# A four-layer image kernel: third layer's gates spread by transfers and computed inside the next half image, 3x3 convolutions as a stage of their own

## The chip, the cores and the metric

The kernel runs on one core of one Trainium2 chip, in one launch. A core has five engines that work side by side, each through its own stream of instructions: PE (TensorE, matmuls, with PEld for the loads of its weights), DVE (VectorE), ACT (ScalarE), POOL (GpSimd) and SP (SyncE, which here only issues transfers). They meet through semaphores. Operands lie in SBUF, matmul results in PSUM, and large tensors in HBM, called DRAM in the code. The metric is the device time of one execution in microseconds (us); of several runs the median is given.

## The reference

Four layers follow each other on a batch of four 64x64 images with 128 channels, in float32. The first (layer 0) and second (layer 1) are vision state-space blocks: projections, a depthwise convolution, and scans over the image in four directions; the first also has a branch with two 3x3 convolutions. The fourth is a 7x7 neighborhood attention. The change lies in the third layer (layer 2 in the code) and in the order of the side work of the first two. The third layer is, cut to its core:

```python
norm = _ln(tokens, ln1_w, ln1_b)
neigh = stack of the 9 shifted images of norm           # 3x3 neighbours, zero at the borders
edge = concatenate([center, neigh, center - neigh, relp], axis=-1)
drive = _mlp(edge, d_w1, d_b1, d_w2, d_b2)[..., 0]       # gelu between the two products
resistance = _mlp(edge, r_w1, r_b1, r_w2, r_b2)[..., 0]
gate = sigmoid(clip(lam * drive / (softplus(resistance) + softplus(gamma) + 1e-6), -3, 3) + bias)
values = neigh @ v_w + v_b
message = sum(gate * values, axis=2) / sum(gate, axis=2)
return _ln(tokens + message @ o_w + o_b, ln2_w, ln2_b)
```

## The kernel before, in words

Channels lie on the 128 partitions and pixels along the free dimension. An image has 4096 pixels, in eight chunks of 512 (eight rows). A matmul of 128x512 fills one of PSUM's eight banks.

**Layers 0 and 1.** `Scans.run` walks through 3072 units of scan. A unit is one scan on DVE (`scan`) with its decay (PE and ACT), its product with B (POOL, `times_b`), its product with C (DVE) and sums on PE. All other work of these layers is cut into pieces and slipped between the units: `Side` has a generator per stage (`pre0`, `convs`, `post0`, `pre1`, `post1`) that yields at each piece, `order` lists which stage of which image follows which and before which scan it has to be done, and `between` in `scan_layers` draws pieces from that list at a pace of at least `PACE` = 0.83 per unit, or faster where `PIECES`, the number of pieces that a stage is taken to have, says that a scan would come too early. A piece is only drawn if a small planner (`Plan`, `Lane`) finds room for it on its engine, or if it is late. In the kernel before, `pre0` of the images 1 to 3 holds both the projections with the depthwise convolution (`open0`) and the two 3x3 convolutions (`convs`); image 0's `open0` runs ahead of the scans and its `convs` stand after the three `pre0`.

**Layer 2.** `layer2` records a program by hand; each engine runs it in the order in which it is written. Work goes by half images: image `b`, half `s`, four chunks. `Edges.edges` makes 18 steps for a half: for the drive (m = 0) and the resistance (m = 1) nine neighbours each. A step adds the center's projection `cen` (PSUM, four banks) to the shifted projection of the neighbour `near` (SBUF) in two DVE instructions of 128x1024 (`hid`), passes them through GELU on ACT, and sums over channels on PE into row t of four blocks of 32 partitions (`out0`, `out1`, one bank each). Between steps it calls pieces of other work from the list `side`, spread evenly. After the steps `Edges.gates` turns the two banks into gates in five pieces on DVE and ACT: softplus, division, clip, sigmoid, and the division by the sum of the nine gates (a matmul with `mass`). The first two run alone, the other three mixed with a filling of statistics and projections.

The gates of a half are then used among the steps of the next one, in `Edges.gather`: for each neighbour t and each pair of chunks, PE spreads row t of the gates `g` over all partitions with a matmul against `pick` (L1408), into one of two `mm` banks, DVE multiplies it with the shifted values `vals` (L1414), and POOL adds the product to `acc` (L1418). `vals` is made by `project` with a third matmul per chunk and is kept for two images. The second norm and the store follow (`output` in `gather`, and `finish` one half later). `statistics` and `project` prepare the norm and the projections some chunks ahead; `roots` takes inverse square roots as exp(-0.5 ln) on ACT.

The loops of `layer2`: statistics and projections of the first chunks, then eight halves, then `finish` of the last but one, and gather, roots and `finish` of the last.

Of the kernel before, what the change touches and what calls it, by code (L numbers as in the profile page):

```python
# [531 lines left out]
class Side:  # L532
# [254 lines left out]
    def pre0(self, b):  # L787

        yield from self.open0(b)
        yield from self.convs(b)  # L790

    def open0(self, b):
        nc = self.nc
        wt = self.weights(self.d0a[:, 0 : 3 * P])
        cv12, inp = wt[:, 0:P], wt[0:H, P : 3 * P]
        lo, hi = slice(0, H), slice(H, P)
        x = self.fetch("x", self.x0[b, :, chunk(0)])
        for c in range(NCH):
            yield ("PE", self.landed) if c == 0 else "PE"
            ps = self.bank()  # L800
            nc.tensor.matmul(ps, cv12, x, start=True, stop=True)
            if c + 1 < NCH:
                x = self.fetch("x", self.x0[b, :, chunk(c + 1)])
            yield self.when("TAB", "d0")

            rl = self.tile("d0")
            self.act(rl, ps, AF.Silu, scale=self.cv12g, bias=self.cv12b)
            yield "PE POOL"
            l = self.tile("sq")
            nc.gpsimd.tensor_scalar(l[hi], rl[hi], self.bn0g[hi], self.bn0b[hi], ALU.mult, ALU.add)  # L810
            ps = self.bank()
            nc.tensor.matmul(ps, inp[:, 0:P], rl[lo], start=True, stop=True)
            yield self.when("ACT", "d1")
            xi = self.tile("d1")
            nc.scalar.copy(xi, ps)
            self.store("d1", self.xid[0, b, 0][:, chunk(c)], xi)
            self.store("sq", self.ld[b][0][:, chunk(c)], l[hi])
            yield "PE"
            ps = self.bank()
            nc.tensor.matmul(ps, inp[:, P : 2 * P], rl[lo], start=True, stop=True)  # L820
            yield self.when("TAB", "o")
            sz = self.tile("o")
            self.act(sz, ps, AF.Silu)
            self.store("o", self.szd[0, b, 0][:, chunk(c)], sz)
        yield from self.depthwise(self.dww0, self.dwb0, self.xid[0, b, 0], self.xcd[0, b, 0])

    def convs(self, b):
        nc = self.nc
# [194 lines left out]
PIECES = dict(pre0=157, convs=66, post0=114, pre1=172, post1=290)  # L1023
# [3 lines left out]
def order(nb):  # L1027
# [4 lines left out]
    side = []  # L1032
    for b in range(1, nb):
        side.append(("pre0", b, None, (0, b)))
    side[3:3] = [("convs", 0, None, None), ("post0", 0, (0, 0), None)]
    side.append(("pre1", 0, (0, 0), (1, 0)))
    for b in range(1, nb):
        side += [("post0", b, (0, b), None), ("pre1", b, (0, b), (1, b))]
# [6 lines left out]
def scan_layers(tc, C, nb, x_in, d0, s0, d1, s1, out):  # L1045

    nc = tc.nc
    with ExitStack() as es:
# [48 lines left out]
        with tc.manual_schedule():  # L1097
            for _ in side.open0(0):
                pass
# [20 lines left out]
class Edges:  # L1120
# [9 lines left out]
    def __init__(self, tc, C, es, nb, x_in, x_out, d_w, d_rel, d_v):  # L1130
# [4 lines left out]
        self.psum = es.enter_context(tc.tile_pool(name="l2p", bufs=1, space=PSUM))  # L1135

# [56 lines left out]
        self.pick = wp.tile([P, NB, P], F32, name="pick")  # L1193
        nc.vector.tensor_copy(self.pick, fold[:, 0:NB].unsqueeze(2).to_broadcast([P, NB, P]))
# [20 lines left out]
        self.vals = [[wp.tile([P, HR, PW], F32, name=f"vals{i}{s}") for s in range(2)] for i in range(min(nb, 2))]  # L1215
# [3 lines left out]
        for tiles in self.vals:  # L1219
            for t in tiles:  # L1220
                nc.vector.tensor_copy(t.rearrange("p h w -> p (h w)"), vb.to_broadcast([P, HR * PW]))
# [37 lines left out]
    def project(self, b, c):  # L1259

        nc = self.nc
        n = self.norm[b % 2][:, c, :]
        s, r = divmod(c, 4)

        def scale():
            nc.gpsimd.tensor_mul(n, n, self.rstd[:, c, :])

        def part(i):
            ps = self.bank()
            nc.tensor.matmul(ps, self.vw if i == 2 else self.wnei[:, i, :], n, start=True, stop=True)  # L1270
            tiles = self.vals[b % 2] if i == 2 else self.near[i]
            bias = self.inb[:, i : i + 1]

            def rows(s, first, some):
                to = tiles[s][:, first : first + some.shape[1], 1 : 1 + HW]
                nc.scalar.activation(to, some, AF.Identity, bias=bias)

            rows(s, 1 + r * ROWS, image(ps))


            if c == 3 and i == 2:
                rows(1, 0, image(ps)[:, ROWS - 1 : ROWS, :])
            if c == 4:
                rows(0, HR - 1, image(ps)[:, 0:1, :])

        return [scale] + [lambda i=i: part(i) for i in range(3)]
# [5 lines left out]
    def edges(self, b, s, side):  # L1292

        nc = self.nc
        out = [self.psum.tile([P, T], F32, name="out", tag=f"out{m}", bufs=1) for m in range(2)]
        steps, gone = 2 * NB, 0

        def add_up(m, t, hids):
            for j in range(4):
# [40 lines left out]
    def gates(self, out, logs, half):  # L1340
# [3 lines left out]
        drive, res = out  # L1344

        def one():
            g = half["g"] = self.tile("g", 2)
            d = half["drive"] = self.tile("drive")
            nc.vector.tensor_scalar_add(d, drive, self.db2)
            nc.vector.tensor_scalar_add(g, res, self.rb2)  # L1350
            e = half["e"] = self.tile("inv", 2)
            nc.vector.tensor_scalar_min(e, g, 30.0)
            nc.scalar.activation(e, e, AF.Exp)

        def two():
            g, e = half["g"], half["e"]
            nc.scalar.preload_act_table_set("natural_log_exp_and_others")
            nc.scalar.activation(e, e, AF.Ln, bias=1.0)
            self.roots(logs)
            nc.vector.tensor_max(g, g, e)  # L1360
# [3 lines left out]
        def three():  # L1364
# [3 lines left out]
            nc.vector.tensor_scalar(g, g, -3.0, self.ebias, ALU.max, ALU.add)  # L1368
            nc.scalar.activation(g, g, AF.Exp, scale=-1.0)

        def four():
# [4 lines left out]
        def five():  # L1376
# [3 lines left out]
            inv = self.tile("inv", 2)  # L1380
            nc.vector.tensor_scalar_max(inv, ps, 1e-6)
            nc.vector.reciprocal(inv, inv)
            nc.vector.tensor_mul(g, g, inv)

        return [one, two, three, four, five]
# [7 lines left out]
    def gather(self, b, s, half):  # L1393
# [6 lines left out]

        def gate(t, pair):
            dy, dx = divmod(t, 3)
            js = (2 * pair, 2 * pair + 1)
            gates = []
            for j in js:
                ps = self.bank()
                part = slice(32 * j, 32 * j + 32)
                nc.tensor.matmul(ps, self.pick[part, t, :], half["g"][part, :], start=True, stop=True)  # L1408
                gates.append(ps)
            for j, ps in zip(js, gates):  # L1410
                acc = half["acc"][:, j, :]
                part = acc if t == 0 else self.tile("part", 3)
                row = j * ROWS + dy
                nc.vector.tensor_mul(  # L1414
                    image(part), image(ps), self.vals[b % 2][s][:, row : row + ROWS, dx : dx + HW]
                )
                if t:
                    nc.gpsimd.tensor_add(acc, acc, part)  # L1418
# [23 lines left out]
        out = [begin] + [lambda t=t, pair=pair: gate(t, pair) for pair in range(2) for t in range(NB)]  # L1442
# [25 lines left out]
def layer2(tc, C, nb, x_in, x_out, d_w, d_rel, d_v):  # L1468
    with ExitStack() as es:
# [12 lines left out]
        with tc.manual_schedule():  # L1482
            run(each(E.statistics, 0, range(8)))
            E.roots([E.rstd])
            run(each(E.project, 0, range(6)))
            E.edge_row()
            run(each(E.statistics, 1, range(2)))
            before = last = None
            for b in range(nb):
                for s in range(2):  # L1490
                    side = E.finish(*before) if before else []
                    if last:
                        side = side + E.gather(*last)
                    if s == 0:
                        ahead = merged(each(E.project, b, range(6, 8)), each(E.statistics, b + 1, range(2, 6)))
                    else:
                        ahead = merged(each(E.project, b + 1, range(2, 4)), each(E.statistics, b + 1, range(7, 8)))
                    out = E.edges(b, s, merged(side, ahead))
                    logs = [last[2]["var"]] if last else []
                    if b + 1 < nb:  # L1500
                        logs.append(E.rstd[:, 0:6, :] if s == 0 else E.rstd[:, 6:8, :])
                    before, last = last, (b, s, {})
                    gates = E.gates(out, logs, last[2])
                    run(gates[:2])
                    if s == 0:
                        fill = each(E.statistics, b + 1, [6]) + each(E.project, b + 1, range(2))
                    else:
                        fill = each(E.project, b + 1, range(4, 6)) + each(E.statistics, b + 2, range(2))
                        if b + 1 < nb:
                            fill.insert(4, E.edge_row)  # L1510
                    run(merged(gates[2:], fill))
            run(E.finish(*before))
# [369 lines left out]
```

## Time and profile before

Three runs took 14561.05 to 14575.93 us, with a median of 14571.96. The profile is of one execution of its own.

| | us |
|---|---|
| median of the runs | 14571.96 |
| the profiled execution's own time | 14573.12 |
| its span, from the first to the last instruction | 14571.1 |
| layers 0 and 1, to the last store of the second | 0 to 12004 |
| layer 2, to its last stores | 12004 to 13211 |
| layer 3 | 13211 to the end |
| mean granted TensorE clock | 0.713 of full speed |

Busy time is given by engine; a row's mean is the duration of one instruction, and "idle before" is how long its engine had nothing to do ahead of it, with the instruction that ended this wait. `xN` is a count. A float32 matmul of 128x512 stands in the trace as two records. A line of windows gives busy time of PE, PEld, DVE, ACT and POOL in one stretch of time, with the granted clock and the share and rate of the DMA engines; a line of the timeline merges equal instructions that follow each other and gives start, time from the first to the last, engine, line and tiles.

### The profile page before, as it was taken

To read this page: it belongs to the slowest core of one execution; us is meant where nothing else is said; L and a number is where in the kernel's file an instruction comes from. 1 tells how busy PE (TensorE), PEld (TensorE's weight loads), DVE (VectorE), ACT (ScalarE), POOL (GpSimd) and SP (SyncE) were. 2 spreads that over 40 slices of the span, in tenths; PEclk is the share of its full clock that TensorE was granted. 3 is DMA by queue.
4 is the path that set the end of the run, shared out by engine and by line. 5 is a ranking of instruction groups with operands and counts; after the bars stand their busy time and mean duration, and the time that the engine had idled before them with its cause. 6 is when DMAs were issued, how large, how long until landed. Compare 5 with 4: busy or idle time off the path is not lost. (4 is left out here: it accounts for less than half of the span.)

```text
span 14571.1 us, 125478 instructions
## 1 busy us (share of the span) xinstructions
PE 10679.9 (73%) x36776; PEld 2744.3 (19%) x36776; DVE 12415.6 (85%) x10627; ACT 7822.9 (54%) x9243; POOL 9850.2 (68%) x4742
## 2 busy tenths in 40 slices
PE   5777767767767767777766776677766667777999
PEld 1111111111111111111111111111111122223555
DVE  4999989899999999999999999999999925565666
ACT  3646454466566555556655555555555545543555
POOL 4777777788788878778877888888888833341000
PEclk7666667766667766666667777667766678767999
DMA  6878787788988988898888778788777720002000
GB/s 164 218 201 223 198 213 205 195 223 209 227 220 210 226 206 204 220 224 205 215 208 220 198 196 205 191 204 206 201 195 192 196 75 21 25 13 49 13 14 7
DMA packets 854306, 2489.98 MB, mean 171 GB/s; under 512 B 143095, under 2 KB 164863, under 8 KB 845431
## 3 DMA queue, kind: packets, MB, share of 16 engines
q1 hardware_dynamic: 853623, 2481.97, 67.7%
q8 instruction: 295, 4.83, 0.2%
q14 instruction: 388, 3.18, 0.1%
HBM read 2060.21 MB, written 270.27 MB: 160 GB/s over the span
## 5 line engine op out<-in xcount | busy, mean ns | idle before, releaser
L398 POOL TENSOR_TENSOR dbu<-dub,repB 128x1024 f32<-128x1024 f32 x3072 | 7189.7, 2354 | 1664.8 <-DVE da L418 836.3
L418 DVE TENSOR_TENSOR_SCAN da<-da,state,dbu 128x1024 f32<-128x1024 f32 x2304 | 5414.6, 2350 | 395.6 <-ACT da L408 325.8
L408 ACT ACTIVATE da<-da,av 128x1024 f32<-128x1024 f32 x3072 | 3341.3, 1089 | 3793.2 <-PE da L406 3738.2
L406 PE MATMUL da<-dp,spread 96*128 96x512 bf16 x6144 | 2602.7, 518 | 2940.7 <-DVE hc L430 2913.8
L430 DVE TENSOR_TENSOR hc<-da,repC 128x1024 f32<-128x1024 f32 x3072 | 3740.2, 1218 | 40.5 <-DVE da L418 0.9
L453 PE MATMUL yps<-hc,gather 128*32 128x512 f32 x12288 | 2373.5, 855 | 2.3 <-DVE hc L430 2.3
L418 DVE TENSOR_TENSOR_SCAN da<-da,dbu 128x1024 f32<-128x1024 f32 x768 | 1759.0, 2290 | 325.1 <-POOL dbu L398 203.3
L406 PEld LDWEIGHTS <-spread 96*128 96x128 bf16 x6144 | 475.2, 107 | 6482.0 <-DVE hc L430 4080.0
L98 PE MATMUL ms<-d,wts 128*128 128x512 f32 (+3 forms) x900 | 708.4, 915 | 160.4 <-POOL d L98 122.6
L98 ACT ACT_TABLE_LOAD x600 | 769.8, 1283 | 86.9 <-DMA xcd<-o 70.3
L98 POOL TENSOR_TENSOR delta<-delta,low 128x1024 f32<-128x1024 f32 x192 | 451.9, 2353 | 451.5 <-ACT low L98 447.4
L98 PE MATMUL mp<-xd,dtw 8*128 8x512 f32 (+1 forms) x768 | 674.8, 972 | 74.5 <-DMA xd<-xdd 58.8
L1418 POOL TENSOR_TENSOR acc<-acc,part 128x512 f32<-128x512 f32 x256 | 318.8, 1268 | 341.8 <-DVE part L1414 341.7
L98 ACT CAST parts<-delta 128x1024 bf16<-128x1024 f32 x384 | 399.9, 1042 | 269.2 <-POOL delta L98 254.2
L446 PE MATMUL yps<-y,ident 128*128 128x512 f32 x576 | 518.1, 993 | 2.4 <-ACT y L471 2.2
L453 PEld LDWEIGHTS yps<-hc,gather 128*32 128x32 f32 x12288 | 284.7, 128 | 1191.8 <-issue 1186.1
L98 POOL TENSOR_TENSOR low<-delta,xc 128x1024 f32<-128x1024 f32 x192 | 500.8, 2608 | 2.0
L1662 ACT ACTIVATE s<-s,nmax 128x512 f32<-128x512 f32 x512 | 366.1, 717 | 249.2 <-DVE nmax L1659 244.4
L1329 ACT ACTIVATE hid<-hid,relb 128x1024 f32<-128x1024 f32 x288 | 319.9, 1143 | 325.2 <-DVE hid L1324 322.1
L98 ACT ACTIVATE low<-mp,av 128x512 f32<-128x512 f32 x384 | 263.5, 686 | 401.2 <-PE mp L98 398.7
L1324 DVE TENSOR_TENSOR hid<-cen,near 128x1024 f32<-128x1024 f32 x288 | 336.1, 1216 | 156.1 <-issue 66.6
L98 PE MATMUL ms<-pad,diag 96*32 96x504 f32 (+1 forms) x2304 | 424.9, 831 | 58.7 <-DMA pad<-xid 33.2
(278 smaller groups left out, 11782.8 us busy)
## 6 DMA issues: line engine op xcount, KB each, us to landing
dub<-dud SPq DMA_DIRECT2D x3072, 512.0 KB
dp<-parts SPq DMA_DIRECT2D x2304, 64.0 KB
repB<-xdd SPq DMA_DIRECT2D x192, 512.0 KB
repC<-xdd SPq DMA_DIRECT2D x192, 512.0 KB
dud<-low SPq DMA_DIRECT2D x192, 512.0 KB
pad<-xid SPq DMA_DIRECT2D x192, 256.0 KB
szd<-o SPq DMA_DIRECT2D x96, 256.0 KB
xcd<-o SPq DMA_DIRECT2D x96, 256.0 KB
```

Source lines behind the costliest of these rows:

```text
L98: return call(*args, **kw)
L398: self.nc.gpsimd.tensor_mul(dbu, self.live.pop(("dub", u)), t.prepared[step]["B"])
L406: self.nc.tensor.matmul(da[:, cols], self.C.spread[:, jj, :], dp[:, j, cols], start=True, stop=True)
L408: self.nc.scalar.activation(da, da, AF.Exp, scale=t.W.a[:, at : at + 1])
L418: nc.vector.tensor_tensor_scan(da[:, way], da[:, way], dbu[:, way], 0.0 if step % NSTEP == 0 else t.states[step - 1][:, g : g + 1], ALU.mu ...
L430: nc.vector.tensor_mul(hc, da, t.prepared[step]["C"])
L446: self.nc.tensor.matmul(out, lhs, self.view(rhs, k, c, i, HALVES), start=True, stop=False)
L453: self.nc.tensor.matmul(self.live["yps"][32 * j : 32 * j + 32, cols], self.C.gather[:, jj, :], self.live["hc", v][:, cols], start=False, s ...
L1324: nc.vector.tensor_add(hid.rearrange("p i (r w) -> p (i r) w", w=HW), cen[pair].rearrange("p i (r w) -> p (i r) w", w=HW), self.near[m][s] ...
L1329: nc.scalar.activation(hid, hid, AF.Gelu, bias=self.relb[:, m, t : t + 1])
L1418: nc.gpsimd.tensor_add(acc, acc, part)
L1662: nc.scalar.activation(s[:, i, :], s[:, i, :], AF.Exp, bias=nmax[:, h : h + 1], accum_out=total[:, h : h + 1],)
```

## The change

It has two parts.

**Order of the side work in layers 0 and 1.** `pre0` loses the convolutions for all images; `convs` is a stage of its own for each image and stands ahead of `post0` of that image, without a scan that it must precede.

**Layer 2.**
- Gates: `gates` has six pieces now (`resistance`, `over`, `clamp`, `sigmoid`, `one_over`, `share`). They aren't run after the steps of their own half but as the first pieces of the next half's list, ahead of its other side work (`early`). The banks of `out` are taken when a sum begins and not when the half begins.
- Spreading: `share` stores the gates into DRAM (`gd`, 256 KB). `gather` loads row t of the four blocks from there to all 128 partitions (`spread`, 1 MB, two buffers), one load ahead of its use. The matmuls with `pick` are gone.
- The product is one DVE instruction of 128x1024 for two chunks, from SBUF, and POOL's sum is one of 128x1024. `part` has two buffers of that size for three of half the size. Neighbours are the outer loop and pairs of chunks the inner one.
- Values: a stage `values` makes `vals` for one half, at the end of that half's list, and there is one set of `vals` for two. `project` keeps two matmuls for three.
- Ahead of the first half, four chunks are projected for six and no statistics of the next image are taken; what was done there and in the filling among the gates is done by the lists of the halves.

```diff
@@ class Side
     def pre0(self, b):
-        yield from self.open0(b)
-        yield from self.convs(b)
-
-    def open0(self, b):
         ...
-PIECES = dict(pre0=157, convs=66, post0=114, pre1=172, post1=290)
+PIECES = dict(pre0=81, convs=76, post0=114, pre1=172, post1=290)
@@ def order
-    for b in range(1, nb):
-        side.append(("pre0", b, None, (0, b)))
-    side[3:3] = [("convs", 0, None, None), ("post0", 0, (0, 0), None)]
-    side.append(("pre1", 0, (0, 0), (1, 0)))
-    for b in range(1, nb):
-        side += [("post0", b, (0, b), None), ("pre1", b, (0, b), (1, b))]
+    side = [("pre0", b, None, (0, b)) for b in range(1, nb)]
+    for b in range(nb):
+        side += [("convs", b, None, None), ("post0", b, (0, b), None), ("pre1", b, (0, b), (1, b))]
@@ class Edges, gates
+        def share():
             g = half["g"]
             ps = self.bank()
             nc.tensor.matmul(ps, self.mass, g, start=True, stop=True)
-            inv = self.tile("inv", 2)
+            inv = self.tile("inv")
             nc.vector.tensor_scalar_max(inv, ps, 1e-6)
             nc.vector.reciprocal(inv, inv)
             nc.vector.tensor_mul(g, g, inv)
+            half["gd"] = self.dram.tile([P, T], F32, name="gd", tag="gd", bufs=2)
+            nc.sync.dma_start(out=half["gd"], in_=g)
@@ gather
+        def load(t):
+            gd = half["gd"]
+            spread[t] = self.tile("spread", 2, (P, 4, T))
+            src = bass.AP(gd.tensor, gd.offset + t * T, [[0, P], [32 * T, 4], [1, T]])
+            nc.sync.dma_start(out=spread[t], in_=src)
+
         def gate(t, pair):
+            if pair == 0 and t + 1 < NB:
+                load(t + 1)
             dy, dx = divmod(t, 3)
-            js = (2 * pair, 2 * pair + 1)
-            gates = []
-            for j in js:
-                ps = self.bank()
-                part = slice(32 * j, 32 * j + 32)
-                nc.tensor.matmul(ps, self.pick[part, t, :], half["g"][part, :], start=True, stop=True)
-                gates.append(ps)
-            for j, ps in zip(js, gates):
-                ...
+            js = slice(2 * pair, 2 * pair + 2)
+            acc = half["acc"][:, js, :]
+            part = acc if t == 0 else self.tile("part", 2, (P, 2, T))
+            row = 2 * pair * ROWS + dy
+            nc.vector.tensor_mul(
+                part.rearrange("p i (r w) -> p (i r) w", w=HW),
+                spread[t][:, js, :].rearrange("p i (r w) -> p (i r) w", w=HW),
+                self.vals[s][:, row : row + 2 * ROWS, dx : dx + HW],
+            )
+            if t:
+                nc.gpsimd.tensor_add(acc, acc, part)
@@ layer2
-            run(each(E.project, 0, range(6)))
-            E.edge_row()
-            run(each(E.statistics, 1, range(2)))
+            run(each(E.project, 0, range(4)))
             ...
+                    if s == 0:
+                        early = each(E.project, b, [4]) + [E.edge_row]
+                        ahead = merged(each(E.project, b, range(5, 8)), each(E.statistics, b + 1, range(5)))
+                        second = E.rstd[:, 5:8, :]
+                    else:
+                        early = []
+                        ahead = merged(each(E.project, b + 1, range(4)), each(E.statistics, b + 1, range(5, 8)))
+                        second = E.rstd[:, 0:5, :]
+                    side = E.values(b, s)
                     if last:
+                        ...
+                        early = merged(E.gates(out, last[2], first, second), early)
+                        side = (E.finish(*before) if before else []) + E.gather(*last) + side
+                    out = E.edges(b, s, early + merged(side, ahead))
-            run(E.finish(*before))
+            run(merged(E.gates(out, last[2], [before[2]["var"]], []), E.finish(*before)))
             run(E.gather(*last))
```

## The prediction

> **What bounds the kernel now.** I read the page's busy rows and slices first, to see which stage has which bound.
>
> ```profile
> PE 10679.9 (73%) x36776; PEld 2744.3 (19%) x36776; DVE 12415.6 (85%) x10627; ACT 7822.9 (54%) x9243; POOL 9850.2 (68%) x4742
> ...
> DVE  4999989899999999999999999999999925565666
> ```
>
> DVE is full from slice 1 to slice 31 (the scans, 200 to 11740 us) and only 5 to 6 tenths full in slices 33 to 35, the third layer. Its edges are in the timeline: first constants at 12003.9, first `hid` at 12091.4, last store at 13211: 1207 us. Busy time by half image (windows cut where `g` of L1383 ends, so a window is one half's edges with its gates):
>
> ```profile
> core 0: us, PE busy (x) PEld busy (x) DVE busy (x) ACT busy (x) POOL busy (x), PEclk, DMA share, GB/s
> 12091.00:12168.00 77.00, 60.58 (x207) 15.88 (x206) 57.21 (x50) 62.26 (x67) 10.09 (x9) 0.91 0.06 21
> 12296.00:12442.00 146.00, 116.47 (x309) 33.65 (x308) 81.61 (x87) 76.01 (x82) 65.09 (x54) 0.75 0.07 24
> 12999.00:13123.00 124.00, 87.68 (x252) 23.22 (x250) 82.91 (x87) 58.33 (x59) 49.74 (x40) 0.70 0.09 30
> 13123.00:13211.00 88.00, 65.20 (x96) 22.92 (x96) 24.79 (x37) 11.47 (x14) 48.82 (x40) 0.58 0.04 12
> ```
>
> A half with a gather takes 124 to 146 us, (13123-12168)/7 = 136.4 in the mean, PE being 71 to 80% busy; the half without one took 77. The groups and waits of 12168 to 13123 say why:
>
> ```profile
> L1418 POOL TENSOR_TENSOR acc<-acc,part 128x512 f32<-128x512 f32 x224 | 279.1, 1268 | 315.8 <-DVE part L1414 315.7
> L1408 PE MATMUL mm<-g,pick 32*128 32x512 f32 x504 | 269.8, 943 | 47.7 <-DVE part L1414 42.4 <-DVE acc L1414 5.1
> L1414 DVE TENSOR_TENSOR part<-mm,vals 128x512 f32<-128x512 f32 x224 | 146.5, 687 | 162.1 <-PE mm L1408 161.3 <-POOL acc L1418 0.3
> ```
> ```profile
> POOL acc L1418 <- DVE part L1414: 315.7, 107, 26.8
> DVE part L1414 <- PE mm L1408: 161.3, 118, 3.7
> PEld mm L1408 <- DVE part L1414: 160.4, 104, 2.5
> DVE hid L1324 <- PE out L1300: 48.4, 29, 4.2
> ```
>
> PE spreads a gate, DVE multiplies, PE waits for the two `mm` banks: a ping-pong. POOL is never late (0.3 us). In the half 12296:12442 DVE's timeline splits into 19 us for four steps, 72 for the gather's stretch (12317 to 12389), 20 for the last five, and 34 from the last `hid` (12409) over the gates to the next half.
>
> **What the Trainium skill says.** "SBUF — State Buffer", Who interferes with whom: a DVE instruction with two SBUF inputs contends with a GpSimd instruction that reads SBUF, whoever is first holding the shared pair. The trace agrees; here four POOL multiplies run back to back beside the gates:
>
> ```profile
> 13107.25 5.74 POOL L1452 TENSOR_TENSOR acc<-acc,var 128x512 f32<-128x512 f32 x4 [9.97 <-ACT var L1391]
> 13108.00 1.05 DVE L1366 TENSOR_TENSOR g<-drive,g 128x512 f32<-128x512 f32 x1
> 13109.09 1.37 DVE L1367 TENSOR_SCALAR g<-g,v 128x512 f32<-128x512 f32 x1
> ```
> ```profile
> 12152.35 0.69 DVE L1366 TENSOR_TENSOR g<-drive,g 128x512 f32<-128x512 f32 x1
> 12153.07 0.49 DVE L1367 TENSOR_SCALAR g<-g,v 128x512 f32<-128x512 f32 x1
> ```
>
> Alone the same instructions take 0.69 and 0.49; POOL's four take 5.74 against 4 x 1.27 = 5.08. Neither today's product (PSUM and SBUF) nor `hid` shows this: `hid` stays at 1.21 to 1.23. "DMA: Bandwidth & Descriptors", Rules for kernel authors: a DMA that reads what another wrote must wait for the first one's completion. No run here shows it for `gd`, but it puts two landings in a row behind the last gate. "ScalarE: Activation LUTs", Table sets: functions of other sets cost a table load; the trace has 1.283 us each, three per half.
>
> **The change, part by part.** Times below are for this one execution (span 14571.1, its own time 14573.12); I add the sum to the median of the runs, 14571.96, which is 1.2 below.
>
> *Prologue.* 18 `mm` projections (20.5 us, 12061.9 to 12082.4) become 8 (two for each of four chunks, about 9.5): -11. Statistics of the next image's first chunks (12082 to 12089) move out: -7. Fewer `vals` fills and no `pick` copy (1.35 us) lie in DVE's 66.6 us of idle time before the first `hid` and count nothing; without it they would be some 4 us. **-18.**
>
> *First half.* Its 49 us of edges (12091 to 12140) get 38 pieces for 24: nine more matmuls of about 1.1. 59 us; its 28 us of gates move into the next half and are counted there. 59 - 77 = **-18.**
>
> *A half with a gather.* The built program's order on DVE is: step 0, resistance, over, clamp, step 1, one_over and share, four steps, 18 products of 128x1024 with five steps among them, seven steps. With an odd half's order all gates but share come before step 1.
> - Boundary: last `hid`, two GELUs, its sum, new `cen`: 6 us (5.7 at the change of m, 12112.3 to 12118.0).
> - Gates with steps 0 and 1: hid 2.3; three evictions 1.9; table, exp, ln until 6.1; max, add, reciprocal 4.5; clamp 1.7; hid 2.3; GELUs, a second table, exp 3.3; add, reciprocal 3.8; mass matmul 2.4; 0.69+3.35+0.69: 29 us (24 in the odd order, which waits for ACT less). A fourth table load per half is in it. So the gates are hardly hidden: DVE is in order and waits for its own chain. Before: 34 with no steps, 39 with two.
> - Four steps until the first product: ACT decides, 8 GELUs of 1.14, four stores of 0.8 and three copies: 15. In it `gd` is stored and the first megabyte loaded.
> - The gather. DVE's 18 products read `spread` and `vals`, both SBUF; 16 POOL sums of 128x1024 take 2.354 each (L398, the same shape). By the lock they don't overlap: with two `part` buffers it goes product, product, sum, sum. A product holds the lock for 1024/512 x 0.54 = 1.08 (L1366 above ended 0.54 after POOL's instruction did). 16 x 2.354 + 18 x 1.08 = 57; POOL's own squares (1.04) and scales (1.27) there add 3 to 4: 61. The ten `hid` among them (no second SBUF input) run under the sums. If the lock cost nothing, POOL alone would give 41; I take 61, since tensor_tensor and tensor_scalar both show it.
> - Seven last steps: PE has 25 matmuls and seven sums of 1.05 to 1.94; at today's four us a step plus five value projections, 36.
>
> Heavy half 6+29+15+61+36 = 147 (146, 143 before), odd 6+24+11+60+34 = 135 (140, 139), (3,0) 140 for 135, the first with a gather 134 for 128, the last 128 for 124. Sum 967 against 955: **+12.** PE loses 269.8/7 = 38 us per half, and this isn't on the path any more.
>
> *Tail.* Gates 29 as before, then store `gd` (2.5) and load a megabyte (7): +9.5; the gather 60 instead of 55 (13123.8 to 13178.7): **+15**.
>
> *The loads.* 9 MB per half. Streams of distinct 2 KB rows ran at 355 GB/s (11752 to 11765), loads in which a row is read 16 times (`dub`, 200 to 210) at 240, both with the queues full. `xs` of 256 KB took 3.1 us from issue to use, so about 2.4 are fixed: 5.4 to 6.8 us each plus the issue on SP. New waits: SP for `gd`'s landing and for a free buffer (behind it on SP `xs`, `xo` and the stores; center matmuls on PE wait for `xs`, but a step in the gather lasts 10 us), and DVE for `spread` (behind it `hid`, then ACT and PE). POOL issues no DMA. A buffer comes free after a tap's two products and is needed two taps (14 us) later less 2.2: 11.8, so they are hidden. Nothing here reads a row 128 times; at half the rate, 120 GB/s, a load takes 8.7 us of the queue against 7 per tap.
>
> *Scans.* Side pieces are the same, in another order; the constants of pieces only shift the pace. Counting `dub` loads between the loads of weights: convs took 3.81 to 3.92 us per unit, projection with depthwise of image 1 to 3 3.72, 3.93, 4.00, post0 3.73 to 3.89, pre1 3.72 to 3.84, post1 3.67. Laying these rates on the changed order (starts at unit 8, 134, 246, convs 0 at 350, post0 438, pre1 528, then a set from 751, 1190, 1610, post1 from 2022) gives 11745 for 11750: **-5**, with 40 either way, since a stall at a change of scan (21 us at 2084) hits another stage.
>
> Sum -18-18+12+15-5 = -14; for what the pieces in a row may still cost each other, +2: 14572 - 12 = **14560**, which this measurement can't tell from no change (0.2% is 29 us).
>
> **Rivals.**
> 1. *The lock costs less*, because POOL's gaps take the products or steps cover them. For: POOL is idle 315 us for DVE today. Against: both forms above. A gather at 41: 8 x -20 - 12 = -172, 14400. At half of it 14480. Chance 0.2.
> 2. *Slower: the loads set the pace.* Place: DVE's product waits for `spread`. It decides once a megabyte takes over 7 us of the queue (150 GB/s). For: re-read rows are slower already (240 for 355), and here every partition reads the same 8 KB. Against: 11.8 us of lead. At 120 GB/s 9 x 8.7 = 78: +17 per gather, 8 x 17 - 12 = +124, 14696. Chance 0.32.
> 3. *The convs in the second layer's scans fit worse* or a forced stage stalls: +60, 14620. Against: every stage ends well ahead of its scan in the built order. Chance 0.05.
> 4. *PE's relief counts after all*: the last seven steps at the clock of 0.91 that the first half had (36 to 28): 7 x -8 - 12, 14500. Chance 0.06.
>
> **How the numbers follow.** My case has 0.37, and its own range is 14490 to 14620 (8 us a half, 40 in the scans). It splits 0.1 faster, 0.2 same, 0.07 slower. With rivals 1 and 4 (0.24 faster, 0.02 same) and 2 and 3 slower (0.37): faster 0.34, same 0.22, slower 0.44. The range runs from the middle of rival 1 to just past rival 2: 14430 to 14710; the full relief (14400) and worse pile-ups stay out.
>
> **What would show it.** The gather's POOL sums in pairs with DVE products of 2 to 3.5 us between them: the lock. DVE `part` waiting for DMA `spread`: rival 2. Products of 1.2 us throughout: rival 1. Time from last `hid` to the tenth of the next half near 45 us: the gates' chain. The start of layer four against 13211, and of the third layer against 12004, separate the two parts of the change. I am wrong if the third layer moves by over 80 us.

## The result, and the profile after

The changed kernel takes 14564.95 us (median of 12 runs, 14551.55 to 14585.11), the kernel before beside it 14570.2 (12 runs, 14559.6 to 14578.91): a ratio of 0.9997, with a 95% interval of 0.9989 to 1.0005. No change can be told. The forecast was 14560. Behind this zero stand two effects of about 30 us with opposite signs, and the forecast had neither of them right.

The profiled execution took 14566.03 us with a span of 14564.3. Busy rows of its page, and DVE in 40 slices:

```profile
PE 10420.1 (72%) x36216; PEld 2643.8 (18%) x36216; DVE 12487.0 (86%) x10480; ACT 7833.2 (54%) x9246; POOL 9891.1 (68%) x4614
...
DVE  4999899989999999999998999999999926665666
```

PE has lost 260 us of work (10679.9 before), and the span is shorter by 7. Both ends of the third layer have moved: its first load is issued at 11979.6 for 12005.1, its last store at 13213.6 for 13211.8. So the stages ahead of it are 25 us shorter, and the third layer is 27 us longer (1234.0 for 1206.7). By stage, from the two traces, with what the prediction's parts give for each:

| stage of layer 2 | before | forecast | after |
|---|---|---|---|
| first load to first `hid` | 86.3 | 68 | 68.3 |
| first half, start to start | 77.2 | 59 | 60.0 |
| six halves with a gather, start to start | 830.5 | 838 | 845.6 |
| last half, to its last `hid` | 95.8 | 128 | 129.1 |
| from there to the last store | 117.0 | 132 | 131.0 |
| sum | 1206.8 | 1225 | 1234.0 |

Each row was forecast within 2%, and yet the prediction's sum had the third layer 7 us shorter. The forecast column (each row from the prediction's own terms: 86.3 - 18; 59; 134 + 147 + 135 + 147 + 135 + 140; 128; 117 + 15) adds up to 18 longer. The section on the prediction comes back to this.

In the windows of the changed kernel one even half and the tail look like this (columns as in the windows of before):

```profile
core 0: us, PE busy (x) PEld busy (x) DVE busy (x) ACT busy (x) POOL busy (x), PEclk, DMA share, GB/s
...
12528.00:12676.00 148.00, 78.36 (x234) 20.98 (x233) 93.87 (x68) 74.54 (x86) 64.53 (x32) 0.77 0.34 89
...
13113.00:13214.00 101.00, 18.57 (x24) 5.85 (x24) 34.50 (x20) 12.25 (x14) 53.45 (x24) 0.55 0.43 117
```

PE is now busy for 78 us of a half (116 in the even half shown of before) and the half is no shorter. No engine is full: DVE, with 94 of 148, is nearest. The groups of the stretch from the second half on and DVE's waits in the third layer say what DVE stands for (a waits line gives the sum, the number of times and the longest):

```profile
L1433 POOL TENSOR_TENSOR acc<-acc,part 128x1024 f32<-128x1024 f32 x112 | 302.4, 2713 | 211.4 <-DVE part L1427 211.4
L1325 DVE TENSOR_TENSOR hid<-cen,near 128x1024 f32<-128x1024 f32 x252 | 294.8, 1213 | 155.1 <-PE out L1301 80.1 <-PE cen L1318 74.8
...
L1427 DVE TENSOR_TENSOR part<-spread,vals 128x1024 f32<-128x1024 f32 x112 | 211.3, 1916 | 85.0 <-DMA spread<-gd 50.3 <-POOL acc L1433 33.5 <-POOL norm L1257 1.1
```
```profile
DVE acc L1427 <- DMA spread<-gd: 72.7, 7, 13.5
...
DVE part L1427 <- DMA spread<-gd: 50.3, 21, 3.9
...
DVE part L1427 <- POOL acc L1433: 33.5, 15, 2.2
```

A product that takes 1.22 us by itself takes 1.92 in the mean, POOL's sum 2.71 for 2.354. That is what the prediction called the lock. The ping-pong of PE and DVE is gone (161 us of DVE's waiting). In its place come longer products and a new wait, 123 us for `spread`. The steps wait longer too, 155 us for 82 in the halves with a gather of the kernel before (where DVE waited 40 more for PE's `out` ahead of the gates, for 7 now):

```profile
L1324 DVE TENSOR_TENSOR hid<-cen,near 128x1024 f32<-128x1024 f32 x252 | 294.8, 1216 | 81.9 <-PE out L1300 48.4 <-PE cen L1317 33.6
```

In the tail, where little else runs, the timeline shows both engines taking turns:

```profile
13122.78 2.36 DVE L1427 TENSOR_TENSOR acc<-spread,vals 128x1024 f32<-128x1024 f32 x2 [9.75 <-DMA spread<-gd]
...
13138.16 4.48 DVE L1427 TENSOR_TENSOR part<-spread,vals 128x1024 f32<-128x1024 f32 x2 [2.23 <-POOL acc L1433]
13141.58 5.55 POOL L1433 TENSOR_TENSOR acc<-acc,part 128x1024 f32<-128x1024 f32 x2 [1.16 <-DVE part L1427]
```

Two products without POOL take 2.36 us, with it 4.48. Two sums and the 1.16 us that POOL waits after them make the cycle of 6.71 us per neighbour.

### The profile page after: what moved, and what is told of

Read it like the earlier page. It is cut to its first block, busy times and chain, and to the rows that moved or that the text cites. A ratio compares the mean times of both kernels' runs of the same rounds, so it can differ in the third digit from the quotient of the medians.

```text
span 14564.3 us, 123850 instructions
## 1 busy us (share of the span) xinstructions
PE 10420.1 (72%) x36216; PEld 2643.8 (18%) x36216; DVE 12487.0 (86%) x10480; ACT 7833.2 (54%) x9246; POOL 9891.1 (68%) x4614
## 5 line engine op out<-in xcount | busy, mean ns | idle before, releaser
L98 PE MATMUL ms<-d,wts 128*128 128x512 f32 (+3 forms) x900 | 707.8, 910 | 147.9 <-POOL d L98 111.0
L1433 POOL TENSOR_TENSOR acc<-acc,part 128x1024 f32<-128x1024 f32 x128 | 346.7, 2723 | 245.5 <-DVE part L1427 245.5
```

The costliest lines, as they stand in the source:

```text
L98: return call(*args, **kw)
```

## The experiments

Every kernel ran beside the kernel before on the same chip, and its ratio is to that. The changed kernel's ratio is 0.9997, 5 us under before, and these 5 us are taken into account where an experiment is compared with it. Lengths by stage are from the traces. "Layer 2" is from its first load to its last store: 1206.7 before, 1234.0 after.

### Each part alone

`order_only` is the kernel before with the new lists of side work and the new constants in `PIECES`, `layer2_only` the kernel before with the new third layer.

```diff
 # order_only, against before
+    side = [("pre0", b, None, (0, b)) for b in range(1, nb)]
+    for b in range(nb):
+        side += [("convs", b, None, None), ("post0", b, (0, b), None), ("pre1", b, (0, b), (1, b))]
 ...
 # layer2_only, against before: classes Edges and layer2 of the changed kernel, all else as before
```

> The kernel before with only the new order of the side work in layers 0 and 1; layer 2 as before. Theory A (the 25 us by which layer 2 starts earlier in the changed kernel's trace come from the order): last scan ends near 11718, layer 2 starts near 11980, layer 2 itself 1207 as before, time near 14546. Theory B (the order is worth the 5 us of the prediction, the rest of the 25 differs from run to run): last scan ends near 11737, time near 14566.

> The kernel before with only the new layer 2; order of the side work as before. Theory A (layer 2 by itself costs 27 us, which the order of the side work pays back): first load of layer 2 to its last store 1234 for 1207, time near 14597. Theory B (the new layer 2 is even and the trace's 27 us are one execution's): time near 14570.

The order alone: 14537.58 us for 14570.93, ratio 0.9974 (0.9963 to 0.9984). The third layer alone: 14598.48, ratio 1.0018 (1.0011 to 1.0024). -33.4 and +27.6 add up to -5.8, and both together measured -5.3. Theory A holds in either case: the change is one part that helps and one that costs as much.

The traces agree. With the old order the last scan ends at 11741.9 and 11743.5. In the 12 traces with the new order it ends between 11701.6 and 11726.0, at 11715.3 in the mean: 27 us earlier. Layer 2 has 1203.3 and 1206.7 with the old code, 1234.0 and 1238.1 with the new. The fourth layer, which no edit touches, varies between 1345 and 1359 with no relation to either part, so that the 8.7 us by which it is shorter in the trace after are no effect of the change.

Where the order gains is in DVE's waits over the whole of the scans. First the kernel before, then `order_only`:

```profile
DVE da L418 <- ACT da L408: 438.3, 346, 17.6
DVE da L418 <- POOL dbu L398: 259.5, 42, 186.8
```
```profile
DVE da L418 <- ACT da L408: 371.5, 301, 12.1
DVE da L418 <- POOL dbu L398: 285.1, 59, 187.4
```

67 us less of waiting for ACT's decay, 26 more for POOL's product. By units: up to the 512th scan the two traces are level (2178 us in both); the next 512 take 1958 us with the old order and 1905 with the new; the 1024 after these 3852 and 3867. Of the 53 us won there, 50 fall to the units 513 to 704. In the old order this stretch holds the convolutions of two images in a row (2213 to 2855 us), in the new one none. The stall that ends at 2105 (17.6 us, 6.8 at the same scan with the new order) lies ahead of the 512th scan, where the traces are level, so it isn't the difference. That the convolutions are, and what the constants in `PIECES` add, is not shown.

### The lock: sums that read nothing

```diff
 # pool_writes, against the changed kernel
-                nc.gpsimd.tensor_add(acc, acc, part)
+                for _ in range(3):
+                    nc.gpsimd.memset(part, 0.0)
```

> The changed kernel with each of POOL's sums replaced by three memsets of the same part buffer (0.88 us each by the trace's fill of 2244 columns in 1.98), so POOL waits for the same products, is as long busy, and hands the buffer back as before, but reads nothing; the messages are not summed (acc keeps the first neighbour). Theory lock (DVE's products wait while POOL reads SBUF): products fall from 1.85 to 1.21 us in the mean, and a gather from 57 to about 48 (9 neighbours of 5.3), about 75 us off the time: 14490. Theory loads (the spread loads set the gather's pace): gather stays at 55 to 58, time 14565.

14518.26 us, ratio 0.9961 (0.9948 to 0.9973): 53 under before, 47 under the changed kernel. Layer 2 is 1186.7. The groups:

```profile
L1434 POOL MEMSET part<- 128x1024 f32 x376 | 352.7, 951 | 200.1 <-DVE part L1427 185.5
L1427 DVE TENSOR_TENSOR part<-spread,vals 128x1024 f32<-128x1024 f32 x126 | 160.7, 1288 | 136.9 <-DMA spread<-gd 73.8 <-POOL part L1434 63.0
```

Three memsets (2.85 us) keep POOL as long as a sum (2.71), and the product falls from 1.92 to 1.29 us. So it is POOL's reading, not its being busy, that stretches the product. The gather falls from 57 to 52 us and not to the 48 expected: DVE's wait for `spread` grows from 50 to 74 us. Taking the lock away wins 47 us in all. (A part may be that the output matmuls no longer wait for POOL's last sum; PE waited 11.8 us for it in the changed kernel.) Behind it, and close, stands the pace of the loads and of POOL's own work.

### The loads: two in place of nine

```diff
 # two_loads, against the changed kernel
             gd = half["gd"]
+            if t > 1:
+                spread[t] = spread[t - 2]
+                return
             spread[t] = self.tile("spread", 2, (P, 4, T))
```

> The changed kernel with two loads of spread in place of nine per half; neighbours 2 to 8 use the two buffers again, so the gates of these neighbours are wrong and seven MB of transfers per half are left out, while DVE and POOL do the same work. Theory lock: the gather keeps eight cycles of 6.7, so falls only from 57 to about 54, 25 us off the time: 14540. Theory loads (the second rival of the prediction: loads set the pace): the gather falls to 45 or less, 100 us or more off: under 14470.

14579.42 us, ratio 1.0003 (0.9995 to 1.0011). With seven of nine megabytes gone, nothing is won, not even what the theory of the lock gave: the gather has 59 us for 57, and layer 2 has 1250.

```profile
L1430 DVE TENSOR_TENSOR part<-spread,vals 128x1024 f32<-128x1024 f32 x112 | 235.3, 2130 | 72.0 <-POOL acc L1436 62.6 <-DMA spread<-gd 9.4
```

The wait for `spread` fell from 50 to 9 us, that for POOL rose from 34 to 63, and the product itself went from 1.92 to 2.13: what a late load had kept DVE from doing was to run into POOL's sum. The rival that the loads set the pace of the gather falls; the wait for a half's first `spread` stays, with 74.4 us. Why the gather even grows by 2 us was not found.

### Loads ahead of the stores

DVE waits for the first `spread` of each half with a gather, 6.6 to 13.5 us; only its waits for `cen` at the boundaries of the halves are as long. The instructions that SP issues in the half from 12528, from the end of the gates to this load, and DVE's first product:

```profile
12558.04 0.32 SPq L1393 DMA_DIRECT2D gd<-g  x1
...
12564.98 7.63 SPq L1472 DMA_DIRECT2D x<-o  x3
12572.71 0.98 SPq L1417 DMA_DIRECT2D spread<-gd  x2
```
```profile
12581.29 2.36 DVE L1427 TENSOR_TENSOR acc<-spread,vals 128x1024 f32<-128x1024 f32 x2 [10.53 <-DMA spread<-gd]
```

`gd` is stored at 12558 and its first load issued at 12573, since `finish` of the half before stands between them on SP with four stores, each of which waits for ACT.

```diff
 # loads_ahead, against the changed kernel
-        out = [begin, lambda: load(0)] + [lambda t=t, pair=pair: gate(t, pair) ...
+        half["ahead"] = [lambda: load(0), lambda: load(1)]
+        out = [begin] + [lambda t=t, pair=pair: gate(t, pair) ...
 ...                     # gate: load(t + 2) after the second product, for load(t + 1) before the first
+                        early += last[2]["ahead"]
```

> The changed kernel with the first two loads of spread issued right after the gates are stored, ahead of the stores of finish, and each later load as soon as both products of its buffer are in the program. Theory queue (the 72.7 us that DVE waits for the first spread of seven gathers come from SP standing at finish's stores, which wait for ACT): first product of an even half starts some 44 us after the half's start for 53, 6 to 10 us per half are won: 14565 - 55 = 14510. Theory steps (the steps' ACT and PE work sets a half's length, and the wait moves to hid): halves stay at 137 to 148, time 14555 to 14565.

14569.81 us, ratio 1.0 (0.9992 to 1.0008), and layer 2 has 1236.5: nothing. The loads are issued 2 us after `gd`, and the first product still starts 54 us after the half's start. SP, PE and DVE in the same half:

```profile
12570.24 0.92 SPq L1417 DMA_DIRECT2D spread<-gd  x2
...
12572.77 1.67 SPq L1229 DMA_DIRECT2D xs<-x  x1
```
```profile
12585.51 2.04 PE L1233 MATMUL mm<-xs,cen 128*128 128x512 f32 x2 [11.87 <-DMA xs<-x]
```
```profile
12589.52 1.23 DVE L1325 TENSOR_TENSOR hid<-cen,near 128x1024 f32<-128x1024 f32 x1 [13.38 <-PE out L1301]
12592.58 2.36 DVE L1425 TENSOR_TENSOR acc<-spread,vals 128x1024 f32<-128x1024 f32 x2 [1.84 <-ACT o L1472]
```

`xs` (256 KB) now goes into the queue behind two megabytes of `spread` and is used 12.7 us after its issue, where it took 3.1 in the kernel before. PE stands at the center matmul that needs it, the sums of the steps stand behind that, and DVE waits 13.4 us for them. The product then waits for ACT besides: `acc` has one buffer, and `finish` still reads it. In the changed kernel the half's first `xs` is issued ahead of the loads and used after 3.5 us; the second goes behind them and is used after 13.1. So the early loads moved this wait ahead of the first product: PE waits for `xs` 39.4 us in the changed kernel (12047 to 12970) and 39.9 here. "DMA: Bandwidth & Descriptors", Queues, rings and completion order, in the Trainium skill says that each DMA engine takes the descriptors of one issuer's ring in their order, though they need not complete in it; the 12.7 us agree with the order. Theory steps was nearer (14555 to 14565), but not for its reason: what holds in this half is the order of `finish`, `xs` and `acc`, not the amount of the steps' work.

### Sums on DVE

```diff
 # sums_dve, against the changed kernel; ahead_dve is loads_ahead with the same edit
-                nc.gpsimd.tensor_add(acc, acc, part)
+                nc.vector.tensor_add(acc, acc, part)
```

> The changed kernel with the sums on DVE in place of POOL. Theory lock: 34 DVE instructions of 1.21 and ten hid of 1.21 make a gather of 53 to 55 for 57, and 45 for 58 in the tail: 14565 - 30 = 14535. Rival (DVE becomes the bound: 16 x 1.21 = 19 us more per half on the engine that is already at 6 to 7 tenths here, and nothing runs beside it): gather 62 or more, time 14600.

> Both edits: loads ahead of finish's stores and sums on DVE. If the queue's wait and the lock are two separate costs, their gains add: -55 and -30, 14480. If one covers the other (a gather that starts earlier waits for something else, or DVE becomes the bound), the sum is less than the larger of the two: 14510 or above.

`sums_dve`: 14549.53 us, ratio 0.9986 (0.9979 to 0.9992), layer 2 1219.3. The gather goes from 57 to 55 us and the tail from 131.0 to 123.6; the product has 1.26 us. Half of what the theory of the lock gave, and on its side: DVE with 34 instructions of the gather and ten steps' `hid` (18 x 1.26 + 16 x 1.25 + 10 x 1.21 = 55) is a little quicker than the two engines taking turns. `ahead_dve`: 14557.92, ratio 0.999 (0.9982 to 0.9998), layer 2 1226.9. The early loads add nothing to it.

### Gates alone again

```diff
 # gates_alone, against the changed kernel
-                        early = merged(E.gates(out, last[2], first, second), early)
+                        run(E.gates(out, last[2], first, second))
```

> The changed kernel with the gates of a half run alone ahead of the next half's steps, in place of being its first pieces. Theory hidden (the two steps among the gates are hidden work: eight us per half): each half with a gather is 6 to 8 us longer, time 14565 + 45 = 14610. Theory chain (DVE stands in its own order in either case, so spreading the pieces among steps lengthens the gates by what it hides): within 15 us of 14565.

14528.76 us, ratio 0.9975 (0.9965 to 0.9985), layer 2 1198.6: 35 us less than with the gates inside the half. Neither theory had this sign. The end of the gates' wait and the steps after them, in the half from 12523:

```profile
12502.16 0.75 DVE L1353 TENSOR_SCALAR g<-out,v 128x512 f32<-128x512 f32 x1 [9.24 <-PE out L1301]
...
12522.92 10.26 DVE L1325 TENSOR_TENSOR hid<-cen,near 128x1024 f32<-128x1024 f32 x9
```

From the first instruction of the gates to their last it is 20.8 us (12502.2 to 12523.0), and the steps then run without a gap. In the changed kernel the same stretch takes 26.9 (12531.1 to 12558.0) with one step in it, and 2.9 of another ahead of it. The waits inside the gates grow, because ACT has the GELUs of a step and a table load after them ahead of its exponentials: 2.04 us for `inv` where it is 0.69 alone, 3.16 for `g` where it is 0.69. At the boundary either kernel waits for PE to work off its queue, 11.2 us for `cen` in the one and 9.2 for `out` in the other. But while the gates run alone, PE computes `cen`, and no step waits for it afterwards. In this half, from last `hid` to first product, that is 58.1 us alone (30.0 and 28.1) for 64.2 inside (11.2 and 53.0).

### Values first

```diff
 # values_first, against the changed kernel
-                    side = E.values(b, s)
 ...
-                    out = E.edges(b, s, early + merged(side, ahead))
+                    out = E.edges(b, s, early + E.values(b, s) + merged(side, ahead))
```

> The changed kernel with the five value projections of a half as the first pieces after the gates, in place of its last ones, so that PE reaches the center projections of the next half with less in its queue. Theory boundary (the 10.7 us from a half's last hid to the next one's first are PE working off value projections): boundary 6 to 7 us, 4 us per half, 14565 - 30 = 14535. Rival (the time only moves: the gather starts later by what the end is shorter): 14560 to 14570.

14532.84 us, ratio 0.9972 (0.996 to 0.9983), layer 2 1209.2. Layer 2 is 25 us shorter, which is the size of the first theory; its mechanism is not the reason: the boundary of the halves with a gather has 7.4 to 12.1 us, 10.1 in the mean for 10.7, and not the 6 to 7 expected. At the end of the half from 12511, PE has matmuls of the norms and outputs in the place of the projections, from the last `hid` (12650.1) to the first `cen` (12657.7). The gain lies in the odd halves (-4 and -5 us), in the first with a gather (-10) and in the two of the last image (-3 and -2); the even halves between change by -0.6 and +1.7. Why these was not settled.

### All of it, in another order

The pieces were then put together by what these runs showed: gates alone, merged with `finish`, so that `acc`, SP and ACT are clear when the half begins; then the first two loads; then the steps with the values first.

```diff
 # best_pool, against loads_ahead; best_dve has the sums on DVE
-                        early = merged(E.gates(out, last[2], first, second), early)
-                        taken = E.gather(*last)
-                        early += last[2]["ahead"]
-                        side = (E.finish(*before) if before else []) + taken + side
+                        run(merged(E.gates(out, last[2], first, second), E.finish(*before) if before else []))
+                        side = E.gather(*last)
+                        run(last[2]["ahead"])
 ...
-                    out = E.edges(b, s, early + merged(side, ahead))
+                    out = E.edges(b, s, early + E.values(b, s) + merged(side, ahead))
```

> The changed kernel with the gates alone between two halves, merged with the scales and stores of finish, then two loads of spread, then the steps, value projections first; sums on POOL. In loads_ahead the first product had to wait for acc, which finish still read, and PE for xs behind finish's stores on SP; here both are out of the way before the first step. Theory: share of the gates to first product 12 us for 22 and a boundary of 27 for 29.5, so 8 to 12 us per half less than with gates alone: 14529 - 70 = 14460. Rival (ACT's steps set a half's length once the gates are out): 14515 to 14530, like gates alone.

> The same with the sums on DVE. With the lock as before: 4 us per gather and 7 in the tail less than the one with sums on POOL, as in the changed kernel, 14440 to 14450. Rival (POOL's sums stand beside nothing else now, DVE is the bound): the same as the one with sums on POOL or slower.

`best_pool`: 14442.7 us, ratio 0.9914 (0.99 to 0.9927). `best_dve`: 14434.88, ratio 0.9906 (0.9892 to 0.9919). Both beat the two kernels of this study, and the order alone. Layer 2 is 1112.5 and 1113.9 us. In `best_pool`, in the even half from 12503, the first product comes 10.2 us after the gates, for 23.3 in the changed kernel (12 expected); the boundary with the gates has 29.9 us, no less than with gates alone (27 expected); the gather still has 57 to 62. A half is 120 to 128 us for 134 to 148. DVE's wait for the first `spread` in `best_pool`, for 72.7 us:

```profile
DVE acc L1425 <- DMA spread<-gd: 24.1, 7, 9.9
```

Sums on DVE gain 9 us in the tail (120.0 for 128.8) and nothing in the halves, where DVE's gather takes 57 to 64 us: the two kernels can't be told apart.

```diff
 # best_split, against best_dve
-                nc.vector.tensor_add(acc, acc, part)
+                add = nc.vector if pair or "final" in half else nc.gpsimd
+                add.tensor_add(acc, acc, part)
```

> The kernel of best_dve with the sums of the first two chunks on POOL and those of the other two on DVE within the halves; in the tail all on DVE. Theory lock (what reads two SBUF inputs on DVE and what POOL does take turns, hid runs beside either): a neighbour costs 2 products and a sum on DVE at 1.08 and one POOL sum of 2.354, 5.6 us, so a gather of 50 to 54 for 57 to 64, 6 us per half less, 14435 - 45 = 14390. Rival (the halves are set by the steps' ACT and PE work by now): the gather shrinks and the steps after it grow by as much, 14425 to 14440.

14438.97 us, ratio 0.9909 (0.9892 to 0.9925): the rival's range. (Its trace has a layer 2 of 1106.3 us, 8 less than `best_dve`, which the runs don't show.) But the lock is seen in it at its plainest. One neighbour on POOL and on DVE:

```profile
12536.36 3.26 POOL L1432 TENSOR_TENSOR acc<-acc,part 128x1024 f32<-128x1024 f32 x1 [4.56 <-DVE part L1425]
```
```profile
12535.07 2.35 DVE L1425 TENSOR_TENSOR part<-spread,vals 128x1024 f32<-128x1024 f32 x2
12537.45 3.25 DVE L1432 TENSOR_TENSOR acc<-acc,part 128x1024 f32<-128x1024 f32 x1
12540.62 2.34 DVE L1325 TENSOR_TENSOR hid<-cen,near 128x1024 f32<-128x1024 f32 x2
```

POOL's sum becomes ready beside the second product and takes 0.9 us longer than its 2.354; DVE's sum then lasts until 1.1 us after POOL's end. The turns take the 5.6 us of the estimate. What failed is that `hid` would run beside POOL: it stands behind DVE's blocked sum, and the cycle of a neighbour with a step is 7.8.

## Why the prediction was right, and where it was not

**The number was right by luck: two errors cancelled.** The forecast total was 12 us below before, 5 were measured. But the third layer was to give 7 of them and gave back 27; the scans were to give 5 and gave 27 to 33.

**The sum of the third layer: an error of 29 us in the books.** The step "Sum 967 against 955" compared two different windows. The 955 run from 12168 to 13123 and hold the gates of the last half, some 29 us. The 967 (its terms add up to 966) are seven halves of the new kernel, the last of which ends with its last `hid`, since its gates have moved to the tail. And the tail's +15 was counted from the last `hid` on in both kernels, so those gates were taken out of one side and put into none. With them -18 - 18 + 12 + 15 + 2 becomes +22. Measured: +27 in the trace, +27.6 by the runs of that part alone.

**Scans: mis-sized.** The step laid rates of 3.67 to 4.00 us per unit on the changed order and got -5 with 40 either way. The order is worth -33 (-23 to -54 by its interval), within that range, and rival 3 had the sign wrong. A mean rate per stage did not find it: 53 us were won in one sixth of the scans.

**Prologue: right. First half: right only as a row of the table.** -18.0 and -17.2 for -18 and -18. But the prediction's 59 us of the first half end with its last `hid`, and its halves run from last `hid` to last `hid`. Counted so, the first half took 52.9 for 59, the next six 842.3 for 838 and the last 139.5 for 128. The added matmuls lengthened the first half's edges by 4 us (48.8 before) and not by 10, and the boundaries are longer than 6; the rows of the table, from first `hid` to first `hid`, even this out.

**A half with a gather: right in its sum, wrong in its parts.** For the even half from 12528 and the odd one from 12390, with the boundary at the end of each:

| part | even: forecast, measured | odd: forecast, measured |
|---|---|---|
| boundary | 6, 10.7 | 6, 11.2 |
| gates with two steps | 29, 29.7 | 24, 25.0 |
| to the first product | 15, 23.3 | 11, 17.3 |
| gather | 61, 57.4 | 60, 57.4 |
| last steps | 36, 26.8 | 34, 27.1 |
| sum | 147, 147.9 | 135, 138.0 |

The boundary was taken from a change of m, where 5.7 us were seen; at the end of this half PE works off other pieces and two sums from 12665.1 to 12674.1 ahead of `cen`, and in the halves with a gather DVE waits 10.1 to 11.2 us. The gates' chain, "hardly hidden", held; what the runs add is that a step inside the gates costs more than one after them, 5 us per half. The lock held: 57 us were its own sum (16 x 2.354 + 18 x 1.08). That the gather meets it so closely is in part chance: DVE also waits 7 us per gather for `spread`, and with the lock gone 52 us are left. The lead of the loads failed in one place, "In it `gd` is stored and the first megabyte loaded": SP's queue was named, but not that the four stores of `finish` stand in it ahead of the first load. And the last steps were costed at four us each plus five value projections; they took 3.8 each with the projections in it. That is the size of rival 4 (36 to 28), but the granted clock, 0.94 and 0.87 in these two stretches, is no higher than in the last steps of before (1.00 and 0.87). With the longer boundary they took 37.5 for 42.

**Tail: right.** +14.0 for +15.

**Rivals.** The first, at full strength 172 us, was wrong even in its size: with the lock taken away the gather has 52 us and not 41, and 47 us are won in all. The second is refuted by `two_loads`. Its place, DVE waiting for `spread`, is there with 123 us, but taking the loads away moves the wait into the products and to POOL. The third went the other way.

## What to carry to other kernels

Before two windows of two kernels are subtracted, mark in both the same first and last instruction; work that moves over a window's edge is lost otherwise. Work of an engine that is in order isn't hidden by putting other work of that engine and of its partners between its pieces: each piece then also waits for the partners' other work (26.9 us for 20.8 in the half shown). When one wait is taken away and the time stays, follow the queues behind it (stores on SP, small loads behind large ones, a single buffer still being read) and move them together: loads ahead, gates alone and values first changed the third layer by +3, -35 and -25 us apart, and by -122 together, with `finish` moved as well. What moving `finish` alone gives was not tried.

## What the runs showed of the hardware

- DVE's instructions on two SBUF tiles and POOL's sums block each other in full and in both directions: a sum on DVE takes 3.25 us for 1.22 when POOL's is ahead, one on POOL 3.26 for 2.354 when DVE's product is. Memsets on POOL, which read nothing, leave the product at 1.29. "SBUF — State Buffer", Who interferes with whom, in the Trainium skill says both, and these numbers agree.
- Giving POOL's 2.354 us sums to DVE at 1.25 gains 2 us per gather only: the `hid` among them, which ran while POOL added up, now add their 1.21 us each.
- A load of 256 KB behind two of 1 MB on the same queue was used 12.7 us after its issue, for 3.1 with nothing ahead of it.
